# Layer 1 of a two-layer graph network: attention weights from the transposed adjacency matrix, in factored form

## The chip, the cores and the metric

One core of one Trainium2 chip runs the whole program. The metric is the device time of one execution in microseconds (us); each run was compared with the kernel before by several executions of both, taken in turns on one chip. A core has a matrix engine (PE, with its weight loads listed apart as PEld), VectorE (DVE), ScalarE (ACT), GpSimd (POOL) and SyncE (SP, which issues DMAs here). "Clock" is the clock granted to PE, as a share of full speed. PSUM is the memory, in banks, into which PE writes its products. A record is one PE entry of the trace; an fp32 product leaves two.

## The reference, cut to what matters

Layer 0 (a top-p attention with a random walk) isn't touched by the change. Layer 1 is a graph attention with four heads over 2708 nodes, an added input and a norm:

```python
Wh = jnp.einsum('nd,hdo->nho', x, W)                # 2708 x 4 x 64
s_i = jnp.einsum('nho,ho->nh', Wh, a_src)
s_j = jnp.einsum('nho,ho->nh', Wh, a_dst)
e = leaky_relu(s_i[:, None, :] + s_j[None, :, :], 0.2)
mask = (adj with ones on the diagonal != 0)[:, :, None]
attention = softmax(where(mask, e, -inf), axis=1)   # over j, the sources
h_prime = einsum('ijh,jho->iho', attention, Wh)
x = layernorm(x + h_prime.reshape(n, 256))
```

The leaky relu is a maximum of z and 0.2 z, so the weight before normalisation is the maximum of exp(s_i + s_j) and exp(0.2 (s_i + s_j)).

## The kernel before: the part that changes

Layer 1 goes by row tiles of 128 nodes i. The weights lie with i in the partitions and j along the free axis, so they have to be turned before a product can sum over j.

```python
for t in range(NT):                                  # 22 row tiles
    bar = adjp.tile([P, N], F32, name="bar")         # 0 or -1e30
    nc.sync.dma_start(bar[:m], adj[t * P : t * P + m, :])
    nc.vector.tensor_scalar(bar[:m], bar[:m], 0.0, NEG,              # L446
                            op0=ALU.is_equal, op1=ALU.mult)
    ...
    for h in range(H):                               # 4 heads
        nc.vector.tensor_tensor_reduce(                              # L458
            y[:m], sj[:m, h, :], bar[:m], 1.0, NEG,
            op0=ALU.add, op1=ALU.max, accum_out=top[:m])
        ...                                          # row max -> two biases
        nc.scalar.activation(e1[:m], y[:m], AF.Exp, bias=bias[:m, 0:1])  # L475
        nc.scalar.activation(y[:m], y[:m], AF.Exp, bias=bias[:m, 1:2],   # L476
                             scale=NEG_SLOPE)
        nc.vector.tensor_tensor(e1[:m], e1[:m], y[:m], op=ALU.max)       # L477
        weigh(ac[:m, h, :], e1, m, ...)   # 22 x: transpose (L138), copy out of
                                          # PSUM (L144), product of 65 columns (L155)
    ...                                   # divide by the sums, add x, norm, store
```

## Time and profile before

The kernel before takes 6774.6 us, the median of three executions (6772.44 to 6775.3).

| stretch (us from the span's start) | length | PE busy | DVE busy | ACT busy | clock |
|---|---|---|---|---|---|
| layer 0, to 5470 | 5470 | | full | | |
| layer 1, set-up, 5470 to 5532 | 62.0 | 46.71 | 37.26 | 30.43 | 1.00 |
| layer 1, main, 5532 to 6771 | 1239.0 | 881.85 | 776.55 | 584.96 | 0.70 |

A row says how long each engine worked within its stretch. An engine that is busy for its whole stretch bounds it. Where none is, as in both stretches of layer 1, the engines wait for each other. Layer 0, four fifths of the time, is bound by DVE alone and cannot change; only the last 1306 us can.

### The profile page before, as it was taken

To read this page: it belongs to the slowest core of one execution; us is meant where nothing else is said; L and a number is where in the kernel's file an instruction comes from. 1 tells how busy PE (TensorE), PEld (TensorE's weight loads), DVE (VectorE), ACT (ScalarE), POOL (GpSimd) and SP (SyncE) were. 2 spreads that over 40 slices of the span, in tenths; PEclk is the share of its full clock that TensorE was granted. 3 is DMA by queue.
4 is the path that set the end of the run, shared out by engine and by line. 5 is a ranking of instruction groups with operands and counts; after the bars stand their busy time and mean duration, and the time that the engine had idled before them with its cause. 6 is when DMAs were issued, how large, how long until landed. Compare 5 with 4: busy or idle time off the path is not lost.

```text
span 6776.2 us, 34805 instructions
## 1 busy us (share of the span) xinstructions
PE 2434.9 (36%) x12452; PEld 1970.2 (29%) x12452; DVE 5976.5 (88%) x7217; ACT 1093.3 (16%) x1453; POOL 59.4 (1%) x165
## 2 busy tenths in 40 slices
PE   3321313213132131242332422323223157777776
PEld 2211212112121121131221311212212136666666
DVE  5999999999999999899999999999999966666665
ACT  2100101001010010010000100100001034444444
POOL 0000000000000000000000000000000000000000
PEclk7665656656566565665665655656656577777776
DMA  1000000000000000000000000000000000000000
GB/s 53 8 17 8 17 8 8 17 8 17 8 8 17 8 10 8 8 17 8 8 17 8 10 15 8 17 8 8 17 8 2 0 25 28 28 28 28 28 28 4
DMA packets 132672, 97.77 MB, mean 14 GB/s; under 512 B 9230, under 2 KB 129662, under 8 KB 129790
## 3 DMA queue, kind: packets, MB, share of 16 engines
q1 hardware_dynamic: 129218, 93.55, 4.8%
q10 hardware_dynamic: 3280, 2.00, 0.1%
q8 instruction: 97, 1.59, 0.1%
q14 instruction: 77, 0.63, 0.0%
HBM read 92.77 MB, written 2.77 MB: 14 GB/s over the span
## 4 chain that ended last, share of the span: by engine, by line
DVE 63%; PE 28%; issue 5%; ACT 2%; DMA 0%; POOL 0%; ACTq 0%; POOLq 0%; SPq 0%; DVEq 0%
DVE scr L241 41%; PE ac L155 13%; PE tr L138 7%; DVE scr L297 4%; PE ac L327 3%; DVE cand L267 3%; DVE hit L263 3%; DVE e L303 2%; DVE same L300 2%; DVE e L273 2%; DVE e L477 2%; PE lg L210 2%; DVE same L279 2%; ACT y L476 2%; PE ac L357 1%
## 5 line engine op out<-in xcount | busy, mean ns | idle before, releaser
L241 DVE SCALAR_TENSOR_TENSOR scr<-e,cand 128x2708 f32<-128x2708 f32 (+1 forms) x1188 | 3609.3, 3038 | 38.1
L138 PE MATMUL tr<-ident,e 128*128 128x128 f32 (+1 forms) x2904 | 564.3, 347 | 4291.9 <-DVE e L303 3934.7
L138 PEld LDWEIGHTS tr<-ident,e 128*128 128x128 f32 (+1 forms) x2904 | 465.9, 189 | 4361.9 <-issue 1991.8
L144 ACT COPY eT<-tr 128x512 f32<-128x512 f32 (+1 forms) x528 | 286.9, 543 | 5049.2 <-PE tr L138 5048.3
L155 PE MATMUL ac<-wh,eT 128*128 128x65 f32 (+3 forms) x3872 | 586.1, 313 | 0.0
L155 PEld LDWEIGHTS ac<-wh,eT 128*128 128x128 f32 (+3 forms) x3872 | 568.2, 228 | 17.0 <-ACT eT L144 9.2
L477 DVE TENSOR_TENSOR e<-e,y 128x2708 f32<-128x2708 f32 (+1 forms) x88 | 258.2, 2975 | 136.0 <-ACT y L476 136.0
L144 DVE COPY eT<-tr 128x512 f32<-128x512 f32 (+3 forms) x264 | 143.1, 542 | 227.9 <-PE tr L138 194.7
L155 PE MATMUL ac<-xa,eT 128*128 128x256 f32 (+1 forms) x968 | 273.1, 432 | 0.0
L155 PE MATMUL ac<-xe,eT 128*128 128x256 f32 (+1 forms) x968 | 264.2, 420 | 0.0
L458 DVE CUSTOM_DVE_ANT_0 y<-sj,bar 128x2708 f32<-128x2708 f32 (+1 forms) x88 | 260.8, 2965 | 0.8 <-ACT sj L439 0.8
L297 DVE TENSOR_TENSOR_SCAN scr<-same 128x2708 f32<-128x2708 bf16 (+1 forms) x44 | 254.8, 5792 | 0.0
L267 DVE SCALAR_TENSOR_TENSOR cand<-hit,bits,cand 128x1 f32<-128x1 f32 (+1 forms) x1012 | 220.9, 218 | 33.5
L263 DVE SCALAR_TENSOR_TENSOR hit<-mass,tau,bits 128x1 f32<-128x1 f32 (+1 forms) x1012 | 220.1, 217 | 31.7
L210 PE MATMUL lg<-kT,qT 64*128 64x512 f32 (+1 forms) x528 | 236.0, 567 | 0.0
L475 ACT ACTIVATE e<-y,bias 128x2708 f32<-128x2708 f32 (+1 forms) x88 | 219.8, 2544 | 50.5 <-DVE bias L470 50.5
L327 PE MATMUL ac<-xe,blk 128*128 128x257 f32 (+1 forms) x968 | 224.1, 385 | 0.6 <-DMA blk<-in_adjT_dram 0.6
L216 DVE TENSOR_REDUCE nmx<-e 128x1 f32<-128x2708 f32 (+1 forms) x44 | 130.8, 2972 | 102.9 <-ACT e L214 102.0
L327 PE MATMUL ac<-xf,blk 128*128 128x256 f32 (+1 forms) x968 | 219.9, 384 | 0.0
L476 ACT ACTIVATE y<-y,bias 128x2708 f32<-128x2708 f32 (+1 forms) x88 | 219.0, 2536 | 0.0
L155 PEld LDWEIGHTS ac<-xa,eT 128*128 128x128 f32 (+1 forms) x968 | 192.7, 211 | 43.2 <-issue 10.0
L155 PEld LDWEIGHTS ac<-xe,eT 128*128 128x128 f32 (+1 forms) x968 | 188.1, 206 | 41.9 <-issue 9.0
(100 smaller groups left out, 2424.5 us busy)
## 6 DMA issues: line engine op xcount, KB each, us to landing
blk<-in_adjT_dram SPq DMA_DIRECT2D x42, 1344.0 KB, 6.7
bar<-in_adj_dram SPq DMA_DIRECT2D x21, 1354.0 KB, 5.7
out_dram<-o SPq DMA_DIRECT2D x21, 128.0 KB, 1.7
xe<-in_x_dram SPq DMA_DIRECT2D x5, 512.0 KB, 5.6
blk<-in_adjT_dram SPq DMA_DIRECT2D x42, 10.0 KB
u_sb<-in_u1T_dram ACTq DMA_DIRECT2D x2, 256.0 KB, 4.8
u_sb<-in_u2T_dram ACTq DMA_DIRECT2D x2, 256.0 KB, 4.7
blk<-in_adjT_dram SPq DMA_DIRECT2D x2, 210.0 KB, 3.4
```

What stands on the lines that cost most here:

```text
L138: nc.tensor.transpose(tr[: rows[t], q, :m], e[:m, t * P : t * P + rows[t]], ident[:m, :m])
L144: copy(eT[:, :full, :m], tr[:, :full, :m])
L155: nc.tensor.matmul(acc, eT[: rows[t], q, :m], value(t), start=(t == 0), stop=(t == NT - 1),)
L210: nc.tensor.matmul(lg[:m, :w], qT[lo:hi, t * P : t * P + m], kT[lo:hi, c0 : c0 + w], start=True, stop=True,)
L241: nc.vector.scalar_tensor_tensor(scr[:m], e[:m], cand[:m], e[:m], op0=ALU.is_ge, op1=ALU.mult, accum_out=mass[:m],)
L263: nc.vector.scalar_tensor_tensor(hit[:m], mass[:m], tau[:m], bits[:m, k : k + 1], op0=ALU.is_ge, op1=ALU.mult,)
L267: nc.vector.scalar_tensor_tensor(cand[:m], hit[:m], bits[:m, low : low + 1], cand[:m], op0=ALU.subtract, op1=ALU.add,)
L297: nc.vector.tensor_tensor_scan(count[:m], same[:m], same[:m], 0.0, op0=ALU.add, op1=ALU.max)
L327: nc.tensor.matmul(ac[:m, :w], blk[: rows[j], j, :m], cur[: rows[j], j, 0:w], start=(j == 0), stop=(j == NT - 1),)
L458: nc.vector.tensor_tensor_reduce(y[:m], sj[:m, h, :], bar[:m], 1.0, NEG, op0=ALU.add, op1=ALU.max, accum_out=top[:m],)
L476: nc.scalar.activation(y[:m], y[:m], AF.Exp, bias=bias[:m, 1:2], scale=NEG_SLOPE)
L477: nc.vector.tensor_tensor(e1[:m], e1[:m], y[:m], op=ALU.max)
```

## The change

The weights are built in transposed form, with the source j in the partitions and 512 targets i along the free axis, so that they can go into a product as the moving operand without being turned. The stationary operand holds the values, 64 columns of a head and one that gives the softmax's sums.

The exponentials are also factored out. Divided by exp(s_i), which cancels in the softmax, the weight is exp(0.2 s_j) times the maximum of b_j = exp(0.8 s_j) and r_i = exp(-0.8 s_i). The factor exp(0.2 s_j) goes into the values. One DVE instruction per source tile, head and chunk of columns then makes the weights: the maximum of r_i with the per-partition scalar b_j, times the edge mask. No row maximum is subtracted, so the kernel counts scores outside of 60 in size and, if there are any, runs the old row form behind a branch. With these inputs there are none.

```diff
-        bar ... tensor_tensor_reduce, two Exp over 2708 columns, max, weigh (per row tile and head)
+            GJ = 4
+            for c0, w in chunks:                  # five of 512 columns, one of 148
+                acc = [ps_a.tile([P, CHUNK], F32, name="pa") for _ in range(H)]
+                for g in range(0, NT, GJ):
+                    edge = adjp.tile([P, GJ, CHUNK], F32, name="edge")
+                    by_tile(edge[:, :, :w], adjT[:, c0 : c0 + w], g, min(g + GJ, NT), g)
+                    nc.vector.tensor_scalar(edge... , 0.0, None, op0=ALU.not_equal)
+                    for q, j in enumerate(js):
+                        ...                        # ones on the diagonal
+                        for h in range(H):
+                            wt = wp_.tile([P, CHUNK], F32, name="wt")
+                            nc.vector.scalar_tensor_tensor(
+                                wt[:m, :w], ri[:m, h, c0 : c0 + w], bj[:m, j, h : h + 1],
+                                edge[:m, q, :w], op0=ALU.max, op1=ALU.mult,
+                            )
+                            nc.tensor.matmul(
+                                acc[h][: FO + 1, :w], wd[:m, j, h, :], wt[:m, :w],
+                                start=(j == 0), stop=(j == NT - 1),
+                            )
+                oT = otp.tile([P, H, CHUNK], F32, name="oT")
+                for h in range(H):
+                    nc.scalar.copy(oT[: FO + 1, h, :w], acc[h][: FO + 1, :w])
+                for t in ...:                      # up to four row tiles of the chunk
+                    ...                            # turn back, divide, add x, norm, store
+    n_bad = nc.values_load(bad[0:1, 0:1], min_val=0, max_val=1 << 20)
+    with tc.If(n_bad > 0):
+        layer1_by_rows()
```

The set-up per tile is rewritten as well: one product now gives the values and the scores together (columns of W joined with W times a), and r_i comes from transposed scores through one exponential of 512 columns.

## The prediction

> **What bounds the kernel now.** I read the page's totals first, then the busy time of layer 1 by stretches, then its groups of instructions, then the order of single instructions where I needed start-to-start times.
>
> ```profile
> DVE  5999999999999999899999999999999966666665
> PEclk7665656656566565665665655656656577777776
> ```
>
> Two stages. In the first 32 slices (169.4 us each) VectorE (DVE) never rests: that is layer 0's top-p search, which the diff touches only in comments. In the last eight slices no engine is full. The boundary is the first layer-1 memset at 5470.0 us; the set-up of layer 1 runs to 5532.0 us, when the first masked row starts. Stretches of the trace (columns: us, then busy us with instruction counts of PE, weight load, DVE, ACT, POOL, then granted clock, DMA share, GB/s):
>
> ```profile
> 5470.00:5532.00 62.00, 46.71 (x238) 28.61 (x236) 37.26 (x102) 30.43 (x90) 1.88 (x5) 1.00 0.12 46
> 5532.00:6771.00 1239.00, 881.85 (x5808) 844.42 (x5808) 776.55 (x1135) 584.96 (x440) 16.55 (x42) 0.70 0.07 24
> ```
>
> So layer 1 is 6776 - 5470 = 1306 us, all that the change can win. In it PE is busy 71% at a mean clock of 0.70, DVE 63%, ACT 47%: a chain of engines that wait for each other. The chain of waits over 5532 to 6776 says so:
>
> ```profile
> by line: PE ac L155 31.9%; PE tr L138 26.9%; issue 15.7%; DVE e L477 10.6%; ACT y L476 9.0%; ACT e L475 1.9%; DVE eT L144 1.0%; DVE y L458 0.7%; DVE eT L146 0.6%; DMA bar<-in_adj_dram 0.5%; ACT eT L144 0.3%; DVE bias L470 0.3%; DVE bar L446
> ```
>
> 59% is the transposing of the weights and the products with 65 moving columns; the rest is the exponentials and the maximum ahead of them. The groups that the costs below rest on:
>
> ```profile
> L477 DVE TENSOR_TENSOR e<-e,y 128x2708 f32<-128x2708 f32 x84 | 246.5, 2976 | 127.3 <-ACT y L476 127.3
> L300 DVE SCALAR_TENSOR_TENSOR same<-scr,need,same 128x2708 bf16<-128x2708 f32 x42 | 127.7, 3040 | 1.5
> L446 DVE TENSOR_SCALAR bar<-bar 128x2708 f32<-128x2708 f32 x21 | 33.0, 1570 | 23.3 <-DMA bar<-in_adj_dram 23.3
> L125 DVE TENSOR_SCALAR o<-res,ln_mv,ln_rs 128x256 f32<-128x256 f32 x21 | 8.7, 413 | 20.9 <-POOL ln_rs L124 20.9
> L144 ACT COPY eT<-tr 128x512 f32<-128x512 f32 x462 | 270.5, 585 | 4756.7 <-PE tr L138 4755.8
> ```
>
> And two orders in time. DVE in layer 0, and PE in the random walk, whose 22 products leave 44 records:
>
> ```profile
> 5234.68 0.21 DVE L263 SCALAR_TENSOR_TENSOR hit<-mass,tau,bits 128x1 f32<-128x1 f32 x1
> 5234.81 0.42 DVE L118 BATCH_NORM_STATS2 ln_st<-hh 128x6 f32<-128x256 f32 x1
> 5235.14 0.20 DVE L267 SCALAR_TENSOR_TENSOR cand<-hit,bits,cand 128x1 f32<-128x1 f32 x1
> ...
> 1427.77 10.02 PE L327 MATMUL ac<-xe,blk 128*128 128x257 f32 x44
> ```
>
> Independent DVE instructions overlap: L263, one column and a per-partition scalar, lasts 0.21 us but its successor starts 0.13 later; L118 has 256 columns (267 ns at 0.96 GHz), and its successor starts 0.33 later. So an independent instruction costs its columns plus about 0.065 us, plus another 0.065 with a scalar read from SBUF. On PE, (10.02 - 0.38)/43 = 224 ns per record of 257 columns.
>
> **What the Trainium skill says.** "VectorE: DVE Perf Modes", section "The perf-mode tier table": two-tensor fp32 operations run at one element a cycle, fp32 `tensor_scalar` in SBUF at two. Agrees: 2708 columns take 2976 ns in L477, 1570 in L446. "FP8 and Floating Point Precision", section "TensorE Precision Notes": true fp32 is four passes through the array. Agrees: two records per product, and 224 ns is 2 x 257 columns at 2.4 GHz (214 ns) and 10 more. "TensorE: Matmul & The Clock Gate", section "Part 1: The HAM clock gate": 1.2 GHz unless the array has been busy, then 2.4. The trace has both states, and shows what wakes it:
>
> ```profile
> 2638.88:2645.90 7.02, 7.02 (x33) 3.01 (x32) 4.55 (x8) 0.26 (x1) 0.00 (x0) 1.00 0.00 0
> 6057.00:6065.00 8.00, 8.00 (x40) 7.92 (x41) 5.04 (x6) 1.02 (x2) 0.00 (x0) 0.50 0.01 2
> ```
>
> Wide moving operands keep the clock at 1.00 even with 20 stationary columns (first row, L327); layer 1's transposes and 65-column products, where weight loads fill the time, stay at 0.50 for 8 us. "Runtime: NRT & Kernel Launch", section "Instruction fetch mechanics": a taken branch breaks sequential prefetch and stalls. The kernel before has no branch, so nothing in its trace prices this.
>
> **The change part by part.** Removed: row maxima, both exponentials over 2708 columns, the maximum (L458, L475 to L477), every weight transpose and its copy out of PSUM (L138, L144). 1239 us go. In their place, for each column chunk (five of 512, one of 148), each of 22 source tiles and 4 heads: one DVE `scalar_tensor_tensor` and one product, 65 stationary columns and 512 moving.
>
> PE: a record of 512 columns is 2 x 512/2.4 + 10 = 437 ns, two a product: 0.874 us. 88 of them make 76.9 us a full chunk. The 65-column weight loads hide: L327's 128-column ones do. The last chunk: 2 x (2 x 148/2.4 + 10) = 0.267 us, 23.5 us.
>
> DVE: 512/0.96 + 130 = 0.663 us, 88 times 58.3. The edge mask at two elements a cycle: 1.067 + 0.065 for four tiles, five times, and two of 0.33: 6.3. The diagonals 0.8. Together 65.4 us a full chunk; the last chunk 88 x 0.284 + 2.2 = 27.3. The closing of four row tiles adds four times some 1.6 us (three operations of 256 columns at 0.33, L125 at 0.32, small ones), 6.4 us. DVE thus needs 72 us a chunk, plus up to 4 x 1.0 us of waiting for POOL in the norm (20.9 us over 21 in L125's row).
>
> PE also has 16 transposes to close a chunk, 0.12 us each: 1.9. So PE, 79 us, should bound the full chunks narrowly, with DVE at 72 to 76, and DVE the last one.
>
> Set-up: 22 tiles took 62 us, 2.66 us each, with DVE waiting 1.25 us a tile on a copy that waits on PE, through two PSUM buffers shared by two uses. Now PE needs six transposes and four records of 264 columns, 6 x 0.13 + 4 x 0.23 = 1.7 us, ACT 1.4 (copy 0.37, two small exponentials, one of 512 at 0.585), DVE 0.5; I take 2.0 us each plus 4 us for the new joined weight matrix: 48 us.
>
> Chunk boundaries: six PSUM banks for four accumulators let two heads of the next chunk start before the old ones are copied out, and the compiler orders DVE work across stages (the trace has layer-1 products of L430 between layer-0's L365 and L366). I allow 3 us of PE stall at each. Tail: last copies, two row tiles and the store, 7 us; the branch on all engines, 6 us, a guess.
>
> Sum, from 5472 us, between the memset and the first product (5470.0 and 5473.8 today): 5472 + 48 + 5 x (76.9 + 1.9 + 3) + 28 + 7 + 6 = 5970 us. Layer 1 goes from 1306 to about 500.
>
> **Rivals.**
>
> 1. The boundaries don't overlap. DVE is in order, and if the closing of four row tiles comes before the next chunk's weights, PE idles for the copies (0.6), transposes, and four chains of 3.1 us (6770.9 to 6774.0 in the trace for one tile), about 14 us, then restarts cold for a few us. Speaking for it: in layer 1 today DVE did idle 1.0 us in each norm, so nothing filled it. Five times 14 more: 6040 us.
> 2. PE stays at half clock. 88 x 1.73 us is 152 us a chunk, 75 more each: about 6350. Against it: the 1.00 above with narrow stationary operands and wide moving ones.
> 3. DVE becomes the bound, because weights that wait for a buffer don't overlap: the full 3040 - 2821 = 219 ns of L300 count, 0.752 us each, 66.2 + 7.1 + 6.4 + 4 = 84 us a chunk: about 6000.
> 4. DMA: 29.3 MB of columns in 2 KB pieces. 1354 KB of rows landed in 5.7 us (L445's issues), and PE needs 1 MB every 14 us with three buffers. Hidden, except that the first block may arrive late.
> 5. The branch costs more than its 6 us: a jump over the whole row form on every engine. Tens of us at the most would be 6000.
>
> **Range and chances.** Perfect boundaries and a free branch give 5470 + 42 + 5 x 79 + 27 + 9 = 5943; all boundaries serial 6040. I take 5930 to 6040. The 2% line is at 6639 us; even a half clock through the whole of layer 1 stays under it, so faster is 0.98.
>
> **What would show it.** Right: layer 1 starts at about 5470; PE is above 90% busy at clock 1.00 in a full chunk; starts of products are 0.87 us apart; DVE has gaps released by PE, 0.66 us between weights. Wrong: PE idle over 5 us at boundaries released by DVE (rival 1); clock near 0.5 (2); PE waiting on DVE for each product, DVE without gaps (3); DVE waiting on the edge blocks (4); a gap over 10 us after the last store (5). A layer 0 that moves by over 10 us would say that the new program was ordered otherwise there.

## The result, and the profile after

The changed kernel takes 6002.4 us, the median of four executions (5999.88 to 6004.35), beside 6773.78 of the kernel before (four executions). The ratio is 0.8859, with a 95% interval of 0.8847 to 0.8872. Ratios here are the mean time of one kernel's runs over that of the other's of the same rounds, so not quite the ratio of the medians. The outputs are correct. The time lies within the predicted range of 5930 to 6040, 32 us above the predicted 5970.

The page's row of DVE and of the clock in 40 slices, now of 150 us each:

```profile
DVE  5999999999999999998999999999999999995998
PEclk7566566665666656656666666666666666657998
```

Layer 0 keeps its full DVE row. Layer 1 is now only the last three and a half slices, and there both DVE and the clock are high, where before eight slices stood between 5 and 7. The four stretches of layer 1 (columns: us, then busy us with instruction counts of PE, weight load, DVE, ACT, POOL, then clock, DMA share, GB/s) are the set-up, the five full chunks, the last chunk of 148 columns, and the tail:

```profile
5467.50:5540.80 73.30, 51.62 (x244) 31.16 (x242) 27.18 (x77) 26.35 (x92) 2.65 (x5) 0.98 0.10 38
5540.80:5951.00 410.20, 395.94 (x949) 126.06 (x948) 367.89 (x587) 11.63 (x20) 15.87 (x32) 0.97 0.21 68
5951.00:5988.10 37.10, 30.21 (x193) 24.27 (x191) 32.08 (x112) 0.97 (x4) 3.19 (x8) 0.82 0.12 34
5988.10:5998.00 9.90, 0.57 (x5) 0.20 (x2) 3.30 (x12) 0.04 (x1) 1.57 (x4) 0.50 0.08 24
```

In the full chunks PE is busy 395.94 of 410.20 us, 96.5%, and DVE 367.89, 90%: from engines that wait for each other, layer 1 has become a stage with PE as its bound and DVE close behind. In the last chunk the order turns: DVE 86%, PE 81%. ACT, which had 585 us before, has 11.63 left. The set-up, 73.30 us, is longer than the 62 us of before.

Two groups of layer 1 take the place of the transposes, copies and exponentials (columns: line, engine, operation, tiles, shapes, count, then busy us and mean ns of one, then idle time before them with the releasers):

```profile
L609 PE MATMUL pa<-wt,wd 128*65 128x512 f32 x840 | 376.4, 608 | 14.3 <-DVE wt L605 14.3
L605 DVE SCALAR_TENSOR_TENSOR wt<-ri,bj,edge 128x512 f32<-128x512 f32 x420 | 301.4, 747 | 22.8 <-PE pa L609 1.1 <-ACT ri L562 0.7
```

840 records are 420 products, two records each. PE idled only 14.3 us before them in all, always for a weight of DVE. A single record lasts 608 ns, but records overlap, so the busy mean isn't the cost. Record starts are 0.43 us apart where PE isn't held up (172 records in 74.17 us from 5540.83, of which the last one lasts 0.59), so a product costs 0.86 us.

The chain of waits of before named the transposes and the narrow products. The chain of the changed kernel can be followed back only to 5876 us, where it ends for want of a recorded releaser, so its shares of the whole span say little. Its piece for the last full chunk is worth reading (start, us, what):

```profile
5876.01 0.65 DVE wt L605
...
5876.70 73.65 PE pa L609 x164
```

For 73.65 us nothing but PE's own products lies on the path. So the chunk's interior costs what PE costs, and only the boundaries between chunks have anything else. The distance from chunk to chunk can be read from the first copy out of PSUM at each end (ACT's timeline: start, us, what, then in brackets its idle time and releaser):

```profile
5697.60 0.58 ACT L615 COPY oT<-pa 65x512 f32<-65x512 f32 x1 [81.98 <-PE pa L609]
...
5780.99 0.58 ACT L615 COPY oT<-pa 65x512 f32<-65x512 f32 x1 [80.23 <-PE pa L609]
```

This pair is 83.4 us apart. Over the first five such copies (5612.46 to 5947.86) the mean distance is 83.85 us. 88 products of 0.86 us are 75.7, so each boundary costs 8.2 us, where the prediction allowed 4.9: 1.9 for 16 closing transposes and 3 of stall. The transposes take only some 1.1 us (0.42, 0.21 and 0.49 to the next product at the first boundary), so the rest is 7 us.

PE just after a chunk's end shows where some of it goes (PE's timeline; products of the new chunk only):

```profile
5616.61 4.14 PE L609 MATMUL pa<-wt,wd 128*65 128x512 f32 x6
...
5621.08 1.88 PE L609 MATMUL pa<-wt,wd 128*65 128x512 f32 x4
5625.47 1.23 PE L609 MATMUL pa<-wt,wd 128*65 128x512 f32 x2 [2.50 <-DVE wt L605]
5627.37 6.96 PE L609 MATMUL pa<-wt,wd 128*65 128x512 f32 x9 [0.68 <-DVE wt L605]
```

There are two losses here. PE waits 2.50 us and 0.68 us for a weight. And nine records in 6.96 us at 5627.37 are 0.77 us each, nearly twice the 0.43 of elsewhere. DVE, in the same time, runs the closing of row tiles:

```profile
5617.64 0.76 DVE L628 TENSOR_TENSOR res<-pt,den 128x256 f32<-128x256 f32 x2
...
5623.95 0.75 DVE L121 BATCH_NORM_STATS2 ln_st<-res 128x6 f32<-128x256 f32 x2
...
5624.69 0.72 DVE L605 SCALAR_TENSOR_TENSOR wt<-ri,bj,edge 128x512 f32<-128x512 f32 x1
```

From 5617.43, where the first reciprocal starts, to 5624.69 DVE makes no weight; only then does the next one come. From 5615.35 on PE runs six products of the new chunk before it waits, as many as the pool of weights has buffers (`wtp`, 6); whether more buffers would cover the block wasn't tried. The clock in two windows of 1 us (columns as above):

```profile
5616.00:5617.00 1.00, 1.00 (x4) 0.45 (x3) 0.79 (x2) 0.00 (x0) 0.00 (x0) 0.51 0.00 0
...
5629.00:5630.00 1.00, 1.00 (x2) 0.30 (x2) 1.00 (x3) 0.00 (x0) 0.00 (x0) 0.50 0.38 128
```

The clock falls to half twice at this boundary, as at the third and the fifth; at the second and the fourth it falls once, at PE's idle time. Here the second dip follows the idle time. The first comes at 5616, while PE is busy for the whole microsecond and had no gap before it; its cause was open.

In the set-up one tile of 22 looks like this:

```profile
5502.54 0.17 DVE L545 COPY sc<-pa 128x8 f32<-128x8 f32 x1 [2.15 <-PE pa L541]
...
5502.76 0.65 PE L559 MATMUL pt<-ident,sc 128*128 128x128 f32 x4 [0.26 <-DVE sc L545]
...
5503.25 0.38 PE L534 MATMUL pt<-ident,xe 128*128 128x128 f32 x2
5503.45 0.60 ACT L562 ACTIVATE ri<-pt 128x512 f32<-128x512 f32 x1 [0.41 <-PE pt L559]
5503.95 0.37 ACT L538 COPY xT<-pt 128x256 f32<-128x256 f32 x1
5504.36 1.16 PE L541 MATMUL pa<-wx,xT 128*128 128x264 f32 x4 [0.73 <-ACT xT L538]
5505.56 0.17 DVE L545 COPY sc<-pa 128x8 f32<-128x8 f32 x1 [2.15 <-PE pa L541]
```

The copy of the scores comes again after 3.02 us. In between, each step waits for the one before: DVE's copy, PE's transposes of the scores, ACT's exponential, ACT's copy of the next tile's input, PE's product. No engine is full.

### The profile page after: what moved, and what is told of

Same layout as the page of the kernel before. It is cut to its first block, busy times and chain, and to the rows that moved or that the text cites. A ratio compares the mean times of both kernels' runs of the same rounds, so it can differ in the third digit from the quotient of the medians.

```text
span 5998.0 us, 24231 instructions
## 1 busy us (share of the span) xinstructions
PE 1983.2 (33%) x7790; PEld 1278.0 (21%) x7790; DVE 5592.1 (93%) x6765; ACT 517.0 (9%) x1039; POOL 63.5 (1%) x166
## 5 line engine op out<-in xcount | busy, mean ns | idle before, releaser
L141 PE MATMUL tr<-ident,e 128*128 128x128 f32 (+1 forms) x968 | 186.2, 334 | 3934.7 <-DVE e L306 3934.7
L141 PEld LDWEIGHTS tr<-ident,e 128*128 128x128 f32 (+1 forms) x968 | 152.4, 178 | 3984.4 <-issue 1990.2
L147 ACT COPY eT<-tr 128x512 f32<-128x512 f32 (+2 forms) x264 | 136.7, 518 | 4447.6 <-PE tr L141 4447.6
L609 PE MATMUL pa<-wt,wd 128*65 128x512 f32 (+3 forms) x1056 | 424.0, 561 | 21.1 <-DVE wt L605 21.1
L605 DVE SCALAR_TENSOR_TENSOR wt<-ri,bj,edge 128x512 f32<-128x512 f32 (+2 forms) x528 | 341.9, 683 | 27.3 <-PE pa L609 3.8
L609 PEld LDWEIGHTS pa<-wt,wd 128*65 128x65 f32 (+1 forms) x1056 | 143.9, 143 | 287.4 <-issue 143.8
L330 PEld LDWEIGHTS ac<-xf,blk 128*128 128x128 f32 (+1 forms) x968 | 176.2, 186 | 38.1 <-issue 11.8
L330 PEld LDWEIGHTS ac<-xe,blk 128*128 128x128 f32 (+1 forms) x968 | 174.4, 185 | 40.2 <-issue 12.3
L217 ACT COPY e<-lg 128x512 f32<-128x512 f32 (+2 forms) x264 | 134.1, 532 | 125.9 <-PE lg L213 125.6
L303 DVE SCALAR_TENSOR_TENSOR same<-scr,need,same 128x2708 bf16<-128x2708 f32 (+1 forms) x44 | 133.7, 3040 | 1.6
```

The source lines that it names most:

```text
L141: nc.tensor.transpose(tr[: rows[t], q, :m], e[:m, t * P : t * P + rows[t]], ident[:m, :m])
L147: copy(eT[:, :full, :m], tr[:, :full, :m])
L217: nc.scalar.copy(e[:m, c0 : c0 + w], lg[:m, :w])
L330: nc.tensor.matmul(ac[:m, :w], blk[: rows[j], j, :m], cur[: rows[j], j, 0:w], start=(j == 0), stop=(j == NT - 1),)
L605: nc.vector.scalar_tensor_tensor(wt[:m, :w], ri[:m, h, c0 : c0 + w], bj[:m, j, h : h + 1], edge[:m, q, :w], op0=ALU.max, op1=ALU.mult,)
L609: nc.tensor.matmul(acc[h][: FO + 1, :w], wd[:m, j, h, :], wt[:m, :w], start=(j == 0), stop=(j == NT - 1),)
```

## The experiments

**The theory** after this reading: PE's products bound the full chunks, and the 32 us of excess come from a serial set-up (25 us), from boundaries in which a block of DVE work and one or two clock dips hold PE up (3 us each more than allowed), and from a last chunk in which DVE also has closings to do. **The rivals:** DVE, not PE, bounds the chunks; the branch costs the difference; and, for the change as a whole, one of its two halves alone (the orientation, or the factored weights) brings nearly all of the gain. Three calls were made, the first on one chip and the other two on another, and each kernel was compared with the kernel before within its call. The kernel before stood at 6776.12, 6776.58 and 6776.68 us in them, so the changed kernel of the first call (6003.22 us, "the base") serves for all three; a difference of a few us from it is not resolved in the later calls. A wait given with an arrow names the releaser.

### The changed kernel again, as the base of the first call

No edit.

> The changed kernel as it is, for the same chip and the same rounds as the variants. Expected 6002 us and a ratio of 0.886 to the kernel before, as in the first comparison.

Measured: 6003.22 us (five executions), ratio 0.8861 [0.8848, 0.8873]. Its chunk distance was 84.6 us, and its set-up ran from 5470.49 to 5541.24. The result repeats.

### Without the branch

```diff
-    n_bad = nc.values_load(bad[0:1, 0:1], min_val=0, max_val=1 << 20)
-    with tc.If(n_bad > 0):
-        layer1_by_rows()
```

> The column form without the read of the flag, the branch and the row form behind it. Theory: the branch costs only what the trace shows after the last store. In the changed kernel the span ends 4.4 us after the last store was issued (5993.6 to 5998.0), in the kernel before 1.9 us after it (6774.3 to 6776.2), so 2 to 3 us are won: 5999 to 6000 us. Rival: reading the flag or fetching past the row form also holds engines earlier, as the prediction's 6 us guess or more would have it: 5996 us or less.

Measured: 6001.15 us, ratio 0.8856 [0.8844, 0.8868], 2 us less than the base with intervals that overlap. The profile is sharper than the times: with the branch the span ends at 6001.3 us and the last store's issue at 5997.04, 4.3 us apart; without it 6002.1 and 5999.95, 2.15 us apart. From layer 1's first memset to the end it is 530.8 us (5470.51 to 6001.3) and 528.6 (5473.46 to 6002.1). The branch, with the read of its flag, costs some 2 us. The rival falls.

### The set-up one tile ahead

The transposes, copy and product of tile t + 1 are issued ahead of tile t's exponentials and transposed scores.

```diff
-            for t in range(NT):
+            def front(t):
                 ...                  # transposes of x, copy, product
+                return wp
+            ahead = front(0)
+            for t in range(NT):
+                m = rows[t]
+                wp = ahead
+                if t + 1 < NT:
+                    ahead = front(t + 1)
```

> Set-up of layer 1 only: the transposes, the copy and the product of tile t+1 are put ahead of the score transposes and exponentials of tile t. Theory: the set-up is slow (3.0 us a tile, 66 us in all, where 2.0 a tile were predicted) because each tile runs as one chain PE, ACT, PE, DVE, PE, ACT with nothing beside it, not because any engine is full. Then tiles come every 1.8 to 2.1 us and 20 to 26 us are won: about 5979 us. Rival: it is work or the two PSUM buffers that bind; then less than 5 us are won.

Measured: 5985.2 us, ratio 0.8834 [0.8822, 0.8846], 18 us less than the base. PE's timeline:

```profile
5495.88 1.06 PE L541 MATMUL pa<-wx,xT 128*128 128x264 f32 x4
...
5498.11 1.06 PE L541 MATMUL pa<-wx,xT 128*128 128x264 f32 x4
```

A tile takes 2.23 us instead of 3.02, and 22 times 0.79 is 17 us: the order of the instructions alone made the set-up serial. It doesn't reach 2.0 us, because PE still waits 0.47 us in each tile for the exponential of 512 columns, which ACT does ahead of the next copy.

### The closings spread over the next chunk

The closing of each row tile (turn back, divide, add, norm, store) is held back, and one of them is issued after each group of four source tiles of the next chunk.

```diff
+            pending = []
 ...
+                    if pending:
+                        pending.pop(0)()
 ...
-                for t in range(c0 // P, (c0 + w + P - 1) // P):
+                def closing(t, oT=oT, c0=c0):
 ...
+                pending = [lambda t=t, f=closing: f(t) for t in range(c0 // P, ...)]
```

> The closing of the four row tiles of a chunk (transposes, division, norm, store) is no longer done at the boundary but one tile after each group of four source tiles of the next chunk. Theory: at a boundary DVE does the closings in a block of some 7 us in which it makes no weights, PE runs dry, falls to half clock and runs slow for some 7 us more; that is why full chunks are 83.8 us apart where 88 products of 0.86 us and the transposes make 77.5. Then chunks come every 78 to 80 us and 16 to 25 us are won: 5977 to 5986 us. Rival 1: the closings' DVE time is what costs (DVE is the bound over the whole chunk): no gain, under 5 us. Rival 2: the PSUM banks or the first edge block hold the next chunk back: no gain either.

Measured: 5987.43 us, ratio 0.8835 [0.8823, 0.8847], 16 us less than the base. Copies start at 5612.87, 5694.56, 5775.91, 5855.36 and 5936.68, so a chunk takes 81.0 us, instead of 84.6 in the base's trace and 83.85 in the first one. The block of closings thus cost some 3 us a boundary. One dip stayed, at each of the five boundaries. Three stretches around the end of the second chunk, with the clock as the third number from the end:

```profile
5694.00:5696.00 2.00, 2.00 (x6) 0.49 (x5) 2.00 (x4) 1.16 (x2) 0.00 (x0) 1.00 0.00 0
5696.50:5703.00 6.50, 6.50 (x8) 1.45 (x7) 5.96 (x9) 1.01 (x2) 0.00 (x0) 0.50 0.49 161
5703.50:5710.00 6.50, 6.50 (x17) 2.12 (x16) 6.18 (x12) 0.00 (x0) 0.00 (x0) 1.00 0.00 0
```

PE is busy throughout all three, and yet only 8 records start in the middle 6.5 us, at clock 0.50, and 17 in the next 6.5. What precedes the dip are the four products of the last source tile, which has only 20 rows; their first weight load starts at 5693.45. The next run tests that.

### The last source tile made full

The missing 108 rows of the last tile are set to zero, and its weights and products run over 128 rows like the others.

```diff
+            nc.gpsimd.memset(wd[:, NF], 0.0)
+            nc.gpsimd.memset(bj[:, NF], 0.0)
 ...
+                    if full < len(js):
+                        nc.gpsimd.memset(edge[:, full, :w], 0.0)
 ...
-                                wt[:m, :w], ri[:m, h, c0 : c0 + w], bj[:m, j, h : h + 1],
+                                wt[:, :w], ri[:, h, c0 : c0 + w], bj[:, j, h : h + 1],
 ...
-                                acc[h][: FO + 1, :w], wd[:m, j, h, :], wt[:m, :w],
+                                acc[h][: FO + 1, :w], wd[:, j, h, :], wt[:, :w],
```

> The last source tile has 20 rows; here its products run over all 128 rows, the other 108 with zero values and a zero mask (same result, same number of instructions, six small memsets more). In the changed kernel, and in the one with spread closings, where PE had no gap before, the clock fell to half some 2 to 3 us after the four products over 20 rows began, for 4 to 8 us, in four of five boundaries. Theory: products over few rows don't count as activity, four of them in a row (3.4 us) let the clock fall, and the half-clock stretch costs 2 to 3.5 us. Then the first of the two dips at each boundary is gone, at 1.00 through the tail products, and 6 to 15 us are won: 5988 to 5997 us. Rival: the dips come from the gaps at the boundary or from the transposes of the closing; then they stay and the time stays within 3 us of 6003.

Measured: 6000.16 us, ratio 0.8855 [0.8843, 0.8867], 3 us less than the base with intervals that overlap, and short of what was expected. The same stretches of this kernel:

```profile
5694.00:5696.00 2.00, 2.00 (x6) 0.65 (x5) 1.85 (x3) 0.00 (x0) 0.00 (x0) 1.00 0.00 0
5696.50:5703.00 6.50, 6.50 (x23) 2.42 (x22) 5.51 (x9) 2.33 (x4) 0.00 (x0) 1.00 0.51 161
```

The first dip is gone at all five boundaries: 1.00 where the kernel above has 0.50. So the products of 20 rows do make the clock fall, and 108 rows of zeros keep it up. (The expectation's "four of five boundaries" is not what the traces have: the dip came at three of five in the changed kernel and at five of five with spread closings. Why not always isn't shown.) But PE, faster now, runs into the block of closings sooner, waits 4.0 us for a weight at the first boundary instead of 2.50 and 0.68, and the second dip remains (5710 to 5714 in this trace). The chunk distance hardly moves (83.3 us): one of two losses alone was removed, and the other grew. The miss says that the two dips can't be priced one by one.

### PE's products made cheap

```diff
-            wd = keep.tile([P, NT, H, FO + 1], F32, name="wd")
+            wd = keep.tile([P, NT, H, FO + 1], BF16, name="wd")
 ...
-                            wt = wp_.tile([P, CHUNK], F32, name="wt")
+                            wt = wp_.tile([P, CHUNK], BF16, name="wt")
```

> Weights and values of the products in bf16: [...]the DVE instructions unchanged in number and length (they only write bf16). The result is a little less exact. Theory: PE bounds the full chunks, with DVE close below, so a PE that takes a quarter of the time uncovers DVE: 88 weights of 0.663, masks 7, closings 6.4 and some 3 us of waiting, 75 to 77 us a chunk instead of 83.8: 5960 to 5972 us. Rival: DVE or the boundaries bound already; then less than 10 us are won. If PE alone mattered, with no DVE limit below it, it would fall towards 5700.

Measured: 5954.1 us, correct, ratio 0.8787 [0.8774, 0.8801], 49 us less than the base and 6 us better than the expected range. Sixty microseconds of its chunks:

```profile
5610.00:5670.00 60.00, 43.81 (x75) 9.90 (x75) 58.16 (x95) 0.00 (x0) 2.66 (x5) 0.50 0.21 66
```

DVE is busy 58.16 of 60 us, and PE 43.81 at half clock, which now costs nothing. A chunk takes 74.8 us. With PE out of the way DVE becomes the bound, and it needs 74.8 us a chunk against 83.85 of the changed kernel. (Each product now leaves one record instead of two. That PE takes a quarter of the time, as the theory has it, wasn't measured: its products come at DVE's pace.)

### DVE's weights made cheap, with a wrong result

Heads 1 and 3 use the weights of heads 0 and 2, so DVE makes half as many; PE does the same products.

```diff
+                            if h % 2 == 0:
-                            wt = wp_.tile([P, CHUNK], F32, name="wt")
-                            nc.vector.scalar_tensor_tensor(...)
+                                wt = wp_.tile([P, CHUNK], F32, name="wt")
+                                nc.vector.scalar_tensor_tensor(...)
```

> Wrong on purpose: heads 1 and 3 use the weights of heads 0 and 2, so DVE makes half of them; PE does the same products. Theory: PE bounds the full chunks, so these go only from 83.8 to what PE needs with its dips, 79 to 81 us; the last chunk, which DVE bounds, falls from 39 to some 28. Together 23 to 35 us: 5968 to 5980 us. Rival: DVE bounds the full chunks; then each falls by much more than 5 us.

Measured: 5975.46 us, ratio 0.8817 [0.8803, 0.883], 28 us less than the base (relative error 0.24, as intended).

```profile
5630.00:5690.00 60.00, 60.00 (x142) 19.23 (x140) 33.27 (x45) 0.00 (x0) 1.10 (x2) 1.00 0.26 81
```

With half of DVE's weights gone, PE is busy 60.00 of 60 us and a chunk still takes 78.9 us. Together the two runs answer the first rival. DVE alone would need 74.8 us a chunk, PE alone 78.9, and the changed kernel has 83.85. PE bounds, DVE is 4 us behind it, and some 5 us a chunk come from the two getting in each other's way.

They also show which engine bounds the last chunk. From the last full chunk's first copy to the last chunk's first copy the changed kernel takes 39.0 us in its first trace and 38.0 as the base, the kernel with light PE 38.3 and this one 32.8: it is DVE, though less came off than the 11 us expected.

The traces let the distance of the full chunks be added up. The clock's loss is 1 minus the clock, summed over windows of 1 us across the first four boundaries and divided by four, and PE's idle time is taken in the same way; it is an estimate, and a little of it lies in PE's idle time. The transposes are those of the first boundary above.

| us a full chunk | 88 products | transposes | clock's loss | PE idle | sum | measured |
|---|---|---|---|---|---|---|
| changed kernel, first trace | 75.7 | 1.1 | 3.4 | 3.6 | 83.8 | 83.85 |
| the same, as the base | 75.7 | 1.1 | 4.3 | 3.3 | 84.4 | 84.6 |
| closings spread | 75.7 | 1.1 | 3.0 | 0.7 | 80.5 | 81.0 |
| last tile full | 75.7 | 1.1 | 2.6 | 4.2 | 83.6 | 83.3 |
| DVE light | 75.7 | 1.1 | 2.1 | 0 | 78.9 | 78.9 |

Spreading the closings takes the idle time away, and the full tile takes clock loss away and gets idle time for it.

### Four PSUM banks instead of six

```diff
-            ps_a = l1.enter_context(tc.tile_pool(name="ps_a", bufs=6, space=PSUM))
+            ps_a = l1.enter_context(tc.tile_pool(name="ps_a", bufs=4, space=PSUM))
```

> Four PSUM banks for the accumulators instead of six, so that no head of the next chunk has a free bank before its old accumulator is copied out. What the prediction assumed (two free banks let the chunks overlap) makes this slower, by 1 to 3 us a boundary: 6008 to 6018 us. Against it: in the trace the copies (0.58 us) follow at the pace of the last four products (0.86 us), so the first bank is free again before the last product ends; then it changes by less than 5 us.

Measured: 6007.59 us, ratio 0.8866 [0.8853, 0.888], 4 us more, with an interval that overlaps the base's. Its trace has a chunk distance of 84.2 us, between the 83.85 and the 84.6 of the two traces of the changed kernel. The two spare banks aren't what keeps the boundaries short. That each head's bank is copied out in time for its first product of the next chunk would explain it, but this run doesn't show that, and it tells too little to price the banks.

### Half of the change: the orientation alone

Columns and transposed adjacency as in the changed kernel, but with the weights from two exponentials on ACT and a maximum and a product on DVE, and without factors.

```diff
-                            nc.vector.scalar_tensor_tensor(wt ..., op0=ALU.max, op1=ALU.mult)
+                            nc.scalar.activation(wt[:m, :w], ri[...], AF.Exp, bias=sc[...])
+                            nc.scalar.activation(e2[:m, :w], ri[...], AF.Exp,
+                                                 bias=bj[...], scale=NEG_SLOPE)
+                            nc.vector.tensor_tensor(wt[:m, :w], wt[:m, :w], e2[:m, :w], op=ALU.max)
+                            nc.vector.tensor_tensor(wt[:m, :w], wt[:m, :w], edge[...], op=ALU.mult)
```

(Here ri holds s_i itself and bj holds 0.2 s_j; the branch is out.)

> One half of the change alone: the column form (weights made where they are needed as moving operand, no transposes), but each weight by two exponentials on ACT, their maximum and the mask on DVE, as the kernel before makes them, instead of the one instruction from max(b_j, r_i). No branch. Theory: the orientation takes the transposes away, but DVE then needs two instructions of 512 columns a weight, 2 x 0.60 us, 105 us a chunk, with masks and closings 118 to 120 where the changed kernel has 83.8, and some 8 more in the last chunk: 6003 + 5 x 35 + 8, about 6185 us (6160 to 6230). Rival: ACT's four exponentials a source tile and their waits set the pace at over 1.3 us a weight: above 6230.

Measured: 6208.25 us, correct, ratio 0.9163 [0.9149, 0.9177], 568 us less than the kernel before and within the expected range. 110 us of it:

```profile
5620.00:5730.00 110.00, 82.39 (x175) 20.83 (x173) 107.44 (x193) 100.96 (x164) 3.85 (x8) 0.92 0.14 46
```

DVE is busy 107.44 of 110 us, 98%, and ACT 92%; PE waits for the weights.

### The other half: factored weights, rows as before

The row form with one maximum-and-mask per head on DVE, no exponential and no row maximum, but still with all transposes and copies.

```diff
-                    nc.vector.tensor_tensor_reduce(y ..., op0=ALU.add, op1=ALU.max, ...)
-                    ...                                   # row max, biases
-                    nc.scalar.activation(e1[:m], y[:m], AF.Exp, bias=bias[:m, 0:1])
-                    nc.scalar.activation(y[:m], y[:m], AF.Exp, bias=bias[:m, 1:2], scale=NEG_SLOPE)
-                    nc.vector.tensor_tensor(e1[:m], e1[:m], y[:m], op=ALU.max)
+                    nc.vector.scalar_tensor_tensor(
+                        e1[:m], sj[:m, h, :], s_src[:m, t, h : h + 1], bar[:m],
+                        op0=ALU.max, op1=ALU.mult)
```

> The other half alone: the row form of the kernel before, with its transposes and 65-column products, but the weights of a row tile and head by one DVE instruction, max(b_j, r_i) times the mask. Theory: 2.95 us of DVE feed 22 transposes and 44 records; from the trace before, at full clock 22 x 0.126 + 44 x 0.119 = 8.0 us a head on PE, at half clock some 14. PE now never waits for exponentials, so it is the bound: 88 x 8.0 = 704 us with the clock up, set-up 66: about 6245 us (6230 to 6300). Rival: weight loads and narrow products don't keep the clock up even when PE never rests; at half clock 88 x 14 us make the time no better than 6600.

Measured: 6210.27 us, correct, ratio 0.9165 [0.9151, 0.9179], 566 us less than the kernel before and 20 us better than the expected range.

```profile
5540.00:6200.00 660.00, 656.85 (x5720) 624.85 (x5720) 469.65 (x599) 148.29 (x260) 70.54 (x42) 0.99 0.13 46
```

PE is busy 656.85 of 660 us, at clock 0.99. A head of a row tile has 66 records (22 transposes, 22 products of two), so 5720 records are 86.7 heads, at 7.6 us each; before, 88 heads took 1239 us, 14.1 each. The same transposes and products that stood at a mean clock of 0.70 run at nearly full clock once PE never has to wait. (The clock fell once, from 6179 to 6192, while PE worked without a gap on the last row tile, with transposes of 20 rows and products of 20 stationary columns; which of them did it isn't shown.)

So neither half brings nearly all of it: each alone takes some 567 us off, both together 773. The halves overlap, because each alone frees the chain of waits and then ends at a full engine: DVE and ACT in one, PE in the other. That rival falls too.

### The parts that helped, put together

The set-up ahead, the spread closings and the full last tile. Besides, the last full chunk and the short one are cut anew, as 384 and 276 columns, so that no chunk of 148 is left to DVE.

```diff
-            for c0, w in chunks:
+            cols = [0, 4, 8, 12, 16, 19, NT]
+            for t0, t1 in zip(cols, cols[1:]):
+                c0, w = t0 * P, min(t1 * P, N) - t0 * P
```

> The changed kernel with the set-up put ahead, the closings spread, the tail products over 128 rows, and chunks of 4, 4, 4, 4, 3 and 3 row tiles instead of five of 4 and one of 2, all in fp32 with the branch kept. Theory: with the closings spread, the tail products are the only thing left that lowers the clock at a boundary, so here the full tail wins the 3.4 us a boundary that the dips cost in the spread form: full chunks every 77 to 79 us instead of 81. Set-up 18 us, spread closings 16, tail 12 to 16, and 5 to 9 for the last chunk, in which DVE was the bound: 5940 to 5958 us. Rival: the dips at the boundaries stay; then about 5960 to 5970.

Measured: 5963.0 us, correct, ratio 0.8799 [0.8787, 0.8811], 40 us less than the base and 5 us short of the expected range. The whole main stage:

```profile
5522.00:5945.00 423.00, 410.53 (x1132) 145.48 (x1133) 384.26 (x697) 12.15 (x24) 25.48 (x44) 1.00 0.22 68
```

The clock is 1.00 from end to end: the tail tile and the block of closings together account for every dip. A full chunk takes 78 to 81 us. What is missed is a number of small waits: PE idles 12.2 us for weights, in 17 pieces. Most of it, 12 pieces and 8.7 us, comes just after DVE has stood 0.77 us in a closing, waiting for POOL's part of the norm (at 5663.33, and PE at 5664.46); this cost of spreading wasn't foreseen. The blocks of edges come late too: DVE waits 16.1 us for them, against 5.6 in the changed kernel, but only a few of these waits reach PE (1.89 us up to 5839.65, then 1.33 of PE's). The new cut of the chunks wasn't tried alone.

### The same with bf16 products

```diff
-            wd = keep.tile([P, NT, H, FO + 1], F32, name="wd")
+            wd = keep.tile([P, NT, H, FO + 1], BF16, name="wd")
 ...
-                            wt = wp_.tile([P, CHUNK], F32, name="wt")
+                            wt = wp_.tile([P, CHUNK], BF16, name="wt")
```

> As the last one, with weights and values of the products in bf16. [...]DVE bounds everything: 88 x (2708 columns at 0.96 GHz + 6 x 0.130) = 317 us of weights, 34 of masks, 5 of diagonals, 22 closings of 1.6 = 35, together 391 us after a set-up that ends at 5521, and 10 us of end: 5922 to 5940 us. Rival: with PE at half clock and short products some other wait takes its place; then no faster than the fp32 form.

Measured: 5932.58 us, correct, ratio 0.8755 [0.8744, 0.8766]. It is the fastest version found, 70 us under the changed kernel. Those who want fp32 products have the version above it.

## Why the prediction was right

The predicted time was 32 us low of the median, 28 us low of the profiled span of 5998.0 us. Term by term, from the four stretches:

| term | predicted | measured | difference |
|---|---|---|---|
| start of layer 1 | 5472 | 5467.5 | -4.5 |
| set-up | 48 | 73.3 | +25.3 |
| five full chunks | 409 | 410.2 | +1.2 |
| last chunk | 28 | 37.1 | +9.1 |
| tail and branch | 13 | 9.9 | -3.1 |

**What bounds the new stage: right.** It said that PE at 79 us would narrowly bound the full chunks with DVE at 72 to 76. The runs with one of the two made cheap measured 78.9 and 74.8 us. (PE's 78.9 holds 2.1 us of clock loss that the prediction didn't have, and products and transposes 2 us below the predicted 78.8: that they meet is luck.) This rests on start-to-start times taken from other instructions of the old trace, and those held: 0.86 us a product against the 0.874 predicted, and a weight per 0.66 us where DVE isn't held up (five of them in 3.38 us at 5609.90) against 0.663. In the last chunk, 22 weights of 148 columns in 6.32 us at 5967.85 are 0.288 apiece, against 0.284. From the two widths a column costs DVE 1.02 ns, close to the prediction's 0.96 GHz (1.04 ns), for which it gave no source. Busy means would have misled: a record of the new trace lasts 608 ns in the mean where starts are 430 ns apart, and a weight 747 where they are 660 apart.

**The clock: mostly right.** It was 0.97 in the full chunks, and rival 2 (half clock) fell. Two readings were wrong. The window in which transposes and 65-column products "stay at 0.50" lies just after 7.86 us in which PE idled: PE restarted at 6054.95, was busy without a gap, and had its full clock back some 10.7 us later. It shows a restart after a rest, not what wakes the clock; with factored rows, where PE never waits, the same work ran at 0.99. And 20 stationary columns with 257 moving ones did stay at 1.00 in the old trace, but 20 rows don't: the products of the last source tile brought the clock to half for 3 to 7 us.

**The five full chunks: right by errors that cancel.** The product was 0.014 us cheaper, 1.2 us a chunk. The boundary cost 8.2 us instead of 4.9, but only four of them lie in this stretch, since the fifth falls into the last chunk's. 5 x 75.7 + 4 x 8.2 = 411.3 us, close to the measured 410.2; with four boundaries the prediction would have said 404. Spreading the closings took some 3 us off each boundary, and the combined version removed the dips. So rival 1 (boundaries serial) was partly true: DVE's closings did hold up the weights, for about 7 us, but PE idled 3.2 us of it at the first boundary (2.50 and 0.68) and 3.6 in the mean, not 14.

**The start and the set-up: the mis-sized step.** The start's -4.5 us is scatter of layer 0: layer 1's first memset falls between 5467.06 and 5473.46 in ten traces of the column form, whose layer 0 is the same. "I take 2.0 us each" came from the sum of PE's work per tile, on the assumption that other engines' work would lie beside it. The measured tile took 3.02 us, 22 of the 25 us, because the new steps form one chain through PE, ACT and DVE that nothing overlaps. One tile ahead it took 2.23. The trace of before had given the hint: there, too, the set-up had no full engine (46.71 of 62 us on the busiest).

**The last chunk: a term left out.** The 27.3 us of DVE were right for its own weights, but the closings of the chunk ahead of it, 6.4 us by the prediction's own count, fall into it as well, and DVE is the bound there (5 to 6 us came off with DVE light, with PE light nothing clear of the scatter). Counted with the fifth boundary, which the prediction had put with the full chunks, the miss is 4 us and not 9.

**The branch: right in being small.** It is about 2 us instead of the 6 guessed. DMA (rival 4) stayed hidden: DVE waited 5.6 us in all for edge blocks. DVE as the bound (rival 3) needed weights that don't overlap; they did. By the time alone this rival, at "about 6000" (its terms add up to some 5990), fits the measured 6002 better than the prediction does: only the start times and the two runs tell them apart.

## What to carry to other kernels

Turning the operand order, so that computed weights are moving and the values stationary, removes the transposes, and factoring an exponential out of a maximum removes the exponentials; each alone only moved the bound to another engine, and both together paid. Before a set-up loop is priced by its busiest engine, follow one iteration's result through the engines: if each step needs the one before it and the next iteration's first step is issued last, the price is the length of the chain, and issuing it first takes that off. Where two engines are within a few per cent of each other, a block of other work on the second one starves the first even though neither is full on average, so issue it in pieces.

## What the Trainium skill lacked or had wrong

- "TensorE: Matmul & The Clock Gate", section "Part 1: The HAM clock gate", ties the clock to how busy the array has been in a window of about 3.4 us. It doesn't say that a product over few rows counts as little: four products of 20 rows by 512 columns, some 3.4 us of PE busy without a gap, were followed by 6.5 us at clock 0.50, and such a dip came at all five boundaries of that run. With the same products over 128 rows, 108 of them zeros, the clock was 1.00 there.
- The same page, section "Part 4: PE-mode transpose", says that the full clock doesn't engage for transposes in PE's transpose mode. Here a third of PE's records were transposes, mixed with narrow products, and the clock was 0.99 over 660 us, with PE busy 656.85 of them. No run here had transposes alone, and the trace doesn't say whether these are in that mode, so this limits the statement and doesn't refute it.
- "Runtime: NRT & Kernel Launch", section "Instruction fetch mechanics", warns of a stall at a taken branch but gives no price for the stall. The read of the flag and a jump over a whole second form of layer 1 at the end of the program together cost about 2 us (4.3 us from the last store's issue to the end, 2.15 without it).
